# A written order for the first LayerNorm of a graph layer, part of it on GpSimd

## The chip, the cores and the metric

The kernel runs on one core of one Trainium2 chip. Its time is the device time of one execution in microseconds (us). Three runs of the kernel before took 1614.27, 1614.48 and 1616.7 us; their median, 1614.48 us, is what the change is measured against. A separate execution was profiled; its lines are quoted below.

The engines are named as the profile names them: PE (TensorE, matrix products and transposes), DVE (VectorE), ACT (ScalarE), POOL (GpSimd) and SP (SyncE, which only issues transfers).

## The reference, cut to what matters

```python
xn = _layernorm(x, axis=-1)                      # x: 6250 nodes x 256
x = x + _L0_gnn_ref(xn, src, dst, ...) + _L0_mix_ref(xn[None], ...)[0]
x = x + _L0_ffn_ref(_layernorm(x, axis=-1)[None], ...)[0]      # an LSTM over the 6250 rows

def _L0_gnn_ref(node_feats, src, dst, eps, W1, b1, W2, b2, gamma, beta):
    neigh = jax.ops.segment_sum(node_feats[src], dst, num_segments=n)   # 100000 edges
    h = (1.0 + eps) * node_feats + neigh
    h = jax.nn.relu(h @ W1 + b1) @ W2 + b2
    ...                                           # batch norm over the nodes
```

The mixing branch projects xn to q, k and v, normalizes k and v for each head, forms one 32x32 matrix a head from all nodes, and ends in a two-layer network with GELU.

## The kernel before, in words

**Layout.** The 6250 nodes lie as 125 rows by 50 steps: step s holds the nodes 50c + s. A "row tile" is one step, 125 partitions by 256 features, `xn[:, s, :]`. There are 50 of them.

**The first stage** (the pool `ln1`) does this. The edge lists `src` and `dst` come in on ACT's queue, are cast, transposed on PE and copied out as `si` and `drel` (L250 to L258). `x` comes in by five transfers of ten row tiles on SP's queue (each `move` makes two, of 112 and 13 partitions). Each group of ten is normalized: `bn_stats` and `bn_aggr` on DVE (L274, L275), the reciprocal root by the helper `rsqrt` (a Sqrt on ACT, L103, and a reciprocal with one Newton step on DVE, L105 to L109), the shift (L278), ten activations on ACT (L281), and a write of the group to `xn_d` in memory (L282). Then small DVE work makes, from the edges' first and last targets, the flag `within` and the bases `base_b` and `base_c` (L290 to L330). `to_columns` transposes the normalized tiles on PE, four at a time, and copies them to `xnT`, one half of the features on ACT (L120), the other on DVE (L122). Last come the centring of the k and v weights and their bias (L341 to L345), three products of a row of ones with bias rows (L348 to L352), and a transpose of the q weights (L358, L359). In this stage a scheduler orders the instructions of PE, DVE and ACT by their dependences.

**Between the stages**, L381 copies an index row to `iota_p`, and L383 (ACT) and L384 (DVE) write the nodes' own part, (1 + eps) times xn, into `sums`, one half of the features each: 6250 elements a partition, read in runs of 125 and written 50 elements apart. L386 clears the tail of `sums`.

**The edge stage** runs over the edges behind the first 34 groups, 162 groups of up to four tiles of 128 edges, 646 tiles in all. For each tile POOL issues an indirect gather of 128 rows of `xn_d` (L390) into a buffer `eg`, of which there are ten. For each group DVE makes `here`, the selections (L401); PE multiplies each gathered tile with them (L411, two products, each in two passes, so four records a tile); and DVE adds the result to a window of `sums` (L421). The order on PE, DVE and ACT is the written one here (`manual_schedule`). Into the slots between the products the loop puts other jobs: `count_job` counts the edges of the first 34 groups (its key is made on DVE at L623 and used on PE at L629), `kv_job`, `mix_job`, `gin_job` and so on. Slot 0 works on group 34; the selections of group 35 (slot 1) are asked for within slot 0.

**Afterwards** the batch norm is closed, and the LSTM runs over steps; its `residual` function normalizes one row tile at a time, with a `bn_stats` (L883), a `bn_aggr` (L885), an add (L887) and a power on POOL (L889) in a written order.

**Order of transfers.** Every engine works its own list in order; a transfer whose completion counter is still in use by an earlier transfer waits, and holds what stands behind it on its queue.

Of the kernel before, what the change touches and what calls it, by code (L numbers as in the profile page):

```python
# [23 lines left out]
P = 128  # L24
# [28 lines left out]
GRP = 10  # L53
BANK = 512
# [22 lines left out]
def gps_layer(ctx: ExitStack, tc: tile.TileContext, x, src, dst, cols, rows, kvln, wqkv, mw1, mw2, gw1, gw2,  # L77
# [34 lines left out]
    def to_columns(pool, tiles, dest):  # L112

        w = len(tiles) * NC
        for k in range(KD):
            pt = pool.tile([P, BANK], F32, name="mm")
            for i, t in enumerate(tiles):
                nc.tensor.transpose(pt[:, i * NC:(i + 1) * NC], t[:, k * P:(k + 1) * P], ident[:NC, :NC])
            if k == 0:
                nc.scalar.copy(dest[:, :, k, :], pt[:, :w].rearrange("p (s c) -> p s c", c=NC))  # L120
            else:
                nc.vector.tensor_copy(dest[:, :, k, :], pt[:, :w].rearrange("p (s c) -> p s c", c=NC))  # L122

    def by_step(t):

        return t[:N, :].rearrange("(c s) d -> c s d", s=NS)
# [27 lines left out]
    with ExitStack() as s1:  # L154
# [54 lines left out]
        with tc.tile_pool(name="ln1", bufs=2) as lp, tc.tile_pool(name="ps0", bufs=6, space=PSUM) as ps:  # L209
# [18 lines left out]
            for s0 in range(0, NS, GRP):  # L228
                move(nc.sync, xn[:, s0:s0 + GRP, :], by_step(x)[:, s0:s0 + GRP, :])
            row = lp.tile([1, NROW], F32, name="row", bufs=1)  # L230
            nc.scalar.dma_start(row, rows)
            nc.scalar.dma_start(w_qkv, wqkv.rearrange("(k p) m -> p k m", p=P))
            nc.scalar.dma_start(lnp, bass.AP(tensor=kvln.tensor, offset=kvln.offset,
                                             ap=[[0, P], [2 * D, 2], [1, 2 * D]]))
            nc.scalar.dma_start(w1, mw1.rearrange("(k p) m -> p k m", p=P))
            nc.scalar.dma_start(w2, mw2.rearrange("(k p) m -> p k m", p=P))
            nc.scalar.dma_start(g1, gw1.rearrange("(k p) m -> p k m", p=P))
            nc.scalar.dma_start(g2, gw2.rearrange("(k p) m -> p k m", p=P))
# [5 lines left out]

            nc.gpsimd.memset(counts, 0.0)


            for s, to in zip(tiled, (si, drel)):
                f = late[:, 2 * GE:2 * GE + (FULL + 1) * P].rearrange("p (b e) -> p b e", e=P)
                nc.vector.tensor_copy(f[:, :FULL, :], s[:, :FULL, :])  # L250
                nc.vector.tensor_copy(f[:NE % P, FULL, :], s[:NE % P, FULL, :])
                for b0 in range(0, FULL + 1, 4):
                    pt = ps.tile([P, BANK], F32, name="mm")
                    w = min(NE - b0 * P, BANK)
                    for b in range(b0, min(b0 + 4, FULL + 1)):
                        r = min(P, NE - b * P)
                        nc.tensor.transpose(pt[:, (b - b0) * P:(b - b0) * P + r], f[:r, b, :], ident[:r, :r])
                    nc.vector.tensor_copy(to[:, b0 * P:b0 * P + w], pt[:, :w])  # L258


            ends = lp.tile([P, 2, 2], F32, name="ends", bufs=1)
            for i, op in enumerate((ALU.min, ALU.max)):
                nc.vector.tensor_reduce(ends[:rows_g, i, :], dg[:rows_g], axis=AX.X, op=op)
            rows_c, each = COUNTED // 2, 2 * GT // CT
            pairs = lp.tile([P, 2, each], F32, name="pairs", bufs=1)
            for i, op in enumerate((ALU.min, ALU.max)):
                nc.vector.tensor_reduce(pairs[:rows_c, i, :], flat[:rows_c, :].rearrange("p (j e) -> p j e", j=each),
                                        axis=AX.X, op=op)

            for s0 in range(0, NS, GRP):  # L270
                mv = lp.tile([P, GRP, 2], F32, name="ln_mv")
                for i in range(GRP):
                    st = lp.tile([P, 6], F32, name="ln_st")
                    nc.vector.bn_stats(st[:NC], xn[:NC, s0 + i, :])  # L274
                    nc.vector.bn_aggr(mv[:NC, i, :], st[:NC])  # L275
                rs = rsqrt(lp, mv[:NC, :, 1], [NC, GRP], "ln")
                nc.vector.tensor_copy(ln_rs[:NC, s0:s0 + GRP], rs)
                nc.vector.scalar_tensor_tensor(ln_shift[:NC, s0:s0 + GRP], mv[:NC, :, 0], -1.0, rs, op0=ALU.mult,  # L278
                                               op1=ALU.mult)
                for s in range(s0, s0 + GRP):  # L280
                    nc.scalar.activation(xn[:NC, s, :], xn[:NC, s, :], AF.Identity, bias=ln_shift[:NC, s:s + 1],  # L281
                                         scale=ln_rs[:NC, s:s + 1])  # L282
                move(nc.sync, by_step(xn_d)[:, s0:s0 + GRP, :], xn[:, s0:s0 + GRP, :])

            nc.vector.tensor_scalar(ln_rs[:NC], ln_rs[:NC], 1.0, None, op0=ALU.add)
# [3 lines left out]
            fits = lp.tile([P, 2], F32, name="fits", bufs=1)  # L289
            nc.vector.tensor_sub(fits[:rows_g], ends[:rows_g, 1, :], ends[:rows_g, 0, :])  # L290
            nc.vector.tensor_scalar(fits[:rows_g], fits[:rows_g], float(W), None, op0=ALU.is_lt)
            nc.vector.tensor_mul(place[:rows_g], place[:rows_g], place[:rows_g])
            nc.vector.tensor_scalar(place[:rows_g], place[:rows_g], least(1) - least(0), least(0), op0=ALU.mult,
                                    op1=ALU.add)
            nc.vector.tensor_tensor(place[:rows_g], ends[:rows_g, 0, :], place[:rows_g], op=ALU.is_ge)
            nc.vector.tensor_mul(fits[:rows_g], fits[:rows_g], place[:rows_g])
            fit = lp.tile([P, 1], F32, name="fit", bufs=1)
            nc.vector.tensor_add(fit[:rows_g], fits[:rows_g, 0:1], fits[:rows_g, 1:2])

            fit_c = lp.tile([P, 2, each], F32, name="fit_c", bufs=1)  # L300
            nc.vector.tensor_sub(fit_c[:rows_c, 0, :], pairs[:rows_c, 1, :], pairs[:rows_c, 0, :])
            nc.vector.tensor_scalar(fit_c[:rows_c, 0, :], fit_c[:rows_c, 0, :], float(CW), None, op0=ALU.is_lt)
            nc.vector.tensor_scalar(fit_c[:rows_c, 1, :], pairs[:rows_c, 1, :], float(CN), None, op0=ALU.is_lt)
            nc.vector.tensor_mul(fit_c[:rows_c, 0, :], fit_c[:rows_c, 0, :], fit_c[:rows_c, 1, :])
            nc.vector.reduce_sum(place[:rows_c, 0:1], fit_c[:rows_c, 0, :], axis=AX.X)
            nc.vector.tensor_add(fit[:rows_c], fit[:rows_c], place[:rows_c, 0:1])
            pf = ps.tile([P, BANK], F32, name="mm")
            nc.tensor.matmul(pf[:1, :1], fit[:rows_g], ones[:rows_g, 0:1], start=True, stop=True)
            nc.vector.tensor_copy(within, pf[:1, :1])

            base_b = lp.tile([P, GROUPS], F32, name="base_b", bufs=1)
            for j in range(2):
                b = ends[:rows_g, 0, j:j + 1]
                pb = ps.tile([P, BANK], F32, name="mm")
                nc.tensor.transpose(pb[:, :rows_g], b.to_broadcast([rows_g, P]), ident[:rows_g, :rows_g])
                nc.vector.tensor_copy(base_b.rearrange("p (q j) -> p q j", j=2)[:, :, j], pb[:, :rows_g])
                nc.vector.tensor_copy(base_i.rearrange("p (q j) -> p q j", j=2)[:, :, j], pb[:1, :rows_g])

            base_c = lp.tile([P, PAIRS], F32, name="base_c", bufs=1)
            for j in range(each):  # L320
                b = pairs[:rows_c, 0, j:j + 1]
                pb = ps.tile([P, BANK], F32, name="mm")
                nc.tensor.transpose(pb[:, :rows_c], b.to_broadcast([rows_c, P]), ident[:rows_c, :rows_c])
                nc.vector.tensor_copy(base_c.rearrange("p (q j) -> p q j", j=each)[:, :, j], pb[:, :rows_c])
                nc.vector.tensor_scalar(c_base.rearrange("p (q j) -> p q j", j=each)[:, :, j], pb[:1, :rows_c],
                                        float(CN), None, op0=ALU.min)
            nc.vector.tensor_tensor(c_key.rearrange("p (q t) -> p q t", t=CT),
                                    drel[:, :COUNTED * GT].rearrange("p (q t) -> p q t", t=CT),
                                    base_c[:, :, None].to_broadcast([P, PAIRS, CT]), op=ALU.subtract)
            from_bases(drel, drel, base_b, ALU.subtract)  # L330

            for s0, n in CHUNKS:
                to_columns(ps, [xn[:NC, s, :] for s in range(s0, s0 + n)], xnT[:, s0:s0 + n])

# [827 lines left out]
```

## Time and profile before

| what | us |
|---|---|
| median of three runs | 1614.48 |
| the profiled execution, its own time | 1617.26 |
| its span, first to last instruction | 1615.2 |
| busy PE / DVE / ACT / POOL in the span | 1483.9 / 943.9 / 612.0 / 680.7 |
| the first L281 starts / the last group of L281 starts | 29.75 / 59.77 |
| first gather / last gather starts (L390) | 71.8 / 887.9 |
| PE busy with L411 | 389.1 |

Times in the profile's lists count from the start of the span. A row of the list in order of time gives the start, the duration, the engine, the source line, the operation, what is written from what, the shape, how often it stands there in a row, and, in brackets, how long the engine sat idle before it and what released it. A span of POOL or of a pipelined product is rough to some tens of nanoseconds.

### The profile page before, as it was taken

The numbers are of one execution on the slowest core, as the hardware profiler recorded it, in microseconds if no ns is written. First come the engines' busy times: TensorE is split into PE (matmuls) and PEld (weight loads), VectorE is DVE, ScalarE is ACT, GpSimd is POOL, SyncE is SP. The second block draws the span as 40 slices with busy tenths as digits, with TensorE's granted clock in tenths as the row PEclk, the third lists the DMA queues.
The fourth block names the chain that finished last, engine by engine and source line by source line (L and its number), as shares of the span: only waits on it lengthen the run. The fifth ranks groups of instructions, "written<-read, shape, count | busy, mean of one in ns | idle before, by whom it ended". The sixth has DMA issues, their size and how long they took to land. (4 is left out here: it accounts for less than half of the span.)

```text
span 1615.2 us, 31225 instructions
## 1 busy us (share of the span) xinstructions
PE 1483.9 (92%) x11312; PEld 1388.5 (86%) x11312; DVE 943.9 (58%) x3027; ACT 612.0 (38%) x1867; POOL 680.7 (42%) x714
## 2 busy tenths in 40 slices
PE   1789898999989999999999599999999999999984
PEld 1488788989888999999989599999999998888864
DVE  6789888888742222222222385555555557777777
ACT  2833333343312222233222255445554434444440
POOL 2177777777777777777777000000000000000005
PEclk9799999999999999999999799999999999999996
DMA  9533333333444554444444021111111002233315
GB/s 245 194 105 105 105 104 104 105 102 106 133 137 141 151 156 144 122 119 123 120 123 142 29 90 64 65 65 52 65 65 65 14 1 77 90 92 92 94 45 160
DMA packets 64645, 166.03 MB, mean 103 GB/s; under 512 B 14347, under 2 KB 29436, under 8 KB 63228
## 3 DMA queue, kind: packets, MB, share of 16 engines
q0 software_dynamic: 31008, 84.71, 18.4%
q1 hardware_dynamic: 29822, 75.08, 14.3%
q10 hardware_dynamic: 3648, 4.10, 1.1%
q8 instruction: 93, 1.52, 0.4%
q14 instruction: 74, 0.61, 0.1%
HBM read 130.56 MB, written 33.28 MB: 101 GB/s over the span
## 5 line engine op out<-in xcount | busy, mean ns | idle before, releaser
L390 POOL DMA_INDIRECT eg<-xn_d,si x646 | 620.5, 961 | 257.8 <-issue 99.3
L411 PE MATMUL pg<-here,eg 128*128 128x96 f32 x2584 | 389.1, 276 | 32.5 <-DMA eg<-xn_d,si 30.3
L411 PEld LDWEIGHTS pg<-here,eg 128*128 128x128 f32 x2584 | 358.2, 195 | 63.2 <-DMA eg<-xn_d,si 34.4
L962 ACT ACTIVATE gate<-pg,b_l 128x125 f32<-128x125 f32 x718 | 201.9, 366 | 230.4 <-PE pg L953 229.1
L421 DVE TENSOR_TENSOR sums<-sums,pg 128x192 f32 x162 | 57.3, 353 | 349.3 <-PE pg L411 202.9
L920 PE MATMUL pg<-yT,w_ih 128*128 128x125 f32 x1600 | 188.4, 276 | 0.0
L920 PEld LDWEIGHTS pg<-yT,w_ih 128*128 128x128 f32 x1600 | 184.1, 193 | 0.0
L953 PE MATMUL pg<-sums,w_hh 128*128 128x125 f32 x1568 | 183.1, 275 | 0.0
L953 PEld LDWEIGHTS pg<-sums,w_hh 128*128 128x128 f32 x1568 | 179.0, 192 | 0.0
L889 POOL TENSOR_TENSOR ln_r<-ln_v,minus_half 125x1 f32<-125x1 f32 x50 | 27.4, 552 | 350.9 <-DVE ln_v L887 314.0
L1091 POOL TENSOR_TENSOR xr<-xr,rest_t 125x1024 f32<-125x1024 f32 x8 | 22.9, 2899 | 312.3 <-DVEq L1036 312.3
L953 PE MATMUL pg<-h_w,w_hh 128*128 128x125 f32 x1248 | 145.6, 275 | 0.0
L613 ACT ACTIVATE sums<-mm,vec 128x125 f32<-128x125 f32 x100 | 36.4, 365 | 281.4 <-DVE sums L421 232.8
L953 PEld LDWEIGHTS pg<-h_w,w_hh 128*128 128x128 f32 x1248 | 143.0, 192 | 0.0
L597 PE MATMUL mm<-sums,g 128*128 128x125 f32 x800 | 116.8, 282 | 2.6 <-DVE counts L636 2.5
L608 PE MATMUL mm<-z,g 128*128 128x125 f32 x800 | 115.5, 284 | 0.8 <-DVE stats L614 0.6
L597 PEld LDWEIGHTS mm<-sums,g 128*128 128x128 f32 x800 | 103.8, 195 | 6.0 <-issue 2.3
L441 PE MATMUL mm<-m,xr 128*125 128x256 f32 x400 | 107.8, 395 | 0.6 <-DVE counts L636 0.6
L608 PEld LDWEIGHTS mm<-z,g 128*128 128x128 f32 x800 | 102.6, 197 | 1.2 <-DVE stats L614 0.8
L449 ACT ACTIVATE mm<-kv 125x512 f32<-125x512 f32 x50 | 30.1, 602 | 186.4 <-DVE kv L446 186.4
L968 DVE TENSOR_TENSOR new<-gate,gate 128x125 f32<-128x125 f32 x178 | 51.5, 289 | 65.2 <-ACT gate L962 60.3
L401 DVE TENSOR_TENSOR here<-counts,drel 128x384 f32<-128x384 f32 x162 | 89.4, 552 | 0.0
(238 smaller groups left out, 2164.6 us busy)
## 6 DMA issues: line engine op xcount, KB each, us to landing
x_d<-x_out SPq DMA_DIRECT2D x40, 500.0 KB
x_in<-x_d SPq DMA_DIRECT2D x40, 500.0 KB
eg<-xn_d,si POOLq DMA_INDIRECT x646
counts<-xn_d SPq DMA_DIRECT2D x16, 384.0 KB
xn<-in_x_dram SPq DMA_DIRECT2D x5, 1120.0 KB
xn_d<-xn SPq DMA_DIRECT2D x5, 1120.0 KB
m<-in_x_dram SPq DMA_DIRECT2D x50, 112.0 KB
out_dram<-o SPq DMA_DIRECT2D x12, 448.0 KB
```

The source lines that it names most:

```text
L390: nc.gpsimd.indirect_dma_start(out=g, out_offset=None, in_=xn_d[:], in_offset=bass.IndirectOffsetOnAxis(ap=at, axis=0))
L401: nc.vector.tensor_tensor(here[:, :n, :], iota[:, None, :W].to_broadcast([P, n, W]), drel[:, gi * GT:gi * GT + n, None].to_broadcast([P, n ...
L411: nc.tensor.matmul(pg[:, k, :], g[:, k * P:(k + 1) * P], here[:, i, :], start=(i == 0 and k == 0), stop=(i == n - 1), skip_group_check=True)
L421: nc.vector.tensor_add(window, window, pg)
L441: nc.tensor.matmul(pkv[:r, at], xnT[:, j, k, :], w_qkv[:, k, D:][:, at], start=(k == 0 and half == 0), stop=(k == KD - 1), skip_group_chec ...
L597: nc.tensor.matmul(p1[:, m, :], g1[:, k, m * P:(m + 1) * P], sums[:, k, at], start=(m == 0 and k == 0), stop=(k == KD - 1), skip_group_che ...
L608: nc.tensor.matmul(p2[:, a, :], g2[:, m, a * P:(a + 1) * P], z1[:, m, :], start=(a == 0 and m == 0), stop=(m == 2 * KD - 1), skip_group_ch ...
L613: nc.scalar.activation(sums[:, a, at], p2[:, a, :], AF.Identity, bias=col("gb2", a))
L920: nc.tensor.matmul(pg[:, SLOT[g], :], w_ih[:, k, block(g, a)], yT[:, k, s * NC:(s + 1) * NC], start=(i == 0 and k == 0), stop=False, skip_ ...
L953: nc.tensor.matmul(banks[a][:, SLOT[g], :], w_hh[:, k, block(g, a)], h[:, k, :], start=False, stop=(k == KD - 1), skip_group_check=True)
L962: nc.scalar.activation(gate[g], pg[:, SLOT[g], :], AF.Tanh if g == G else AF.Sigmoid, bias=bias(g, a))
L968: nc.vector.tensor_mul(new, gate[I], gate[G])
```

## The change

- **Groups.** x is loaded and normalized in groups of 10, 10, 10, 10, 5 and 5 row tiles (`LN_GROUPS`) where it was five of 10; each group is one pair of loads and one pair of writes to `xn_d`.
- **Order.** PE, DVE and ACT work this stage, too, in the order in which it is written. `bn_aggr` stands right behind its own `bn_stats`; all the flags, bases, keys and the weights' centring stand behind the last group.
- **Reciprocal root.** v to the power -0.5 on POOL (10 or 5 columns at once), with a Newton step on DVE; ACT's Sqrt and DVE's reciprocal go. One of the four `tensor_reduce` over the edges' targets stands behind each of the first four powers.
- **Normalization.** In a group of ten, ACT does seven tiles and POOL three; in a group of five, ACT four and POOL one.
- **Columns.** `to_columns` copies both halves on ACT. After the second, third and fourth group it is called for the tiles of the groups before; the remaining 22 tiles follow behind the bases.
- **Weights.** `w_qkv` is loaded on SP's queue right behind x; the other five weight loads move from ACT's queue to SP's, behind the last write to `xn_d`.
- **Own part.** It becomes a function that is called after the first gathers and the selections of group 34, inside the written order of the edge stage. ACT does 25 of the 50 steps of one half, DVE the other 25 and all 50 of the second half. In the list of DVE's instructions the selections of group 35 now stand behind it; they stood ahead of it.

```diff
-            if k == 0:
-                nc.scalar.copy(dest[:, :, k, :], pt[:, :w].rearrange("p (s c) -> p s c", c=NC))
-            else:
-                nc.vector.tensor_copy(dest[:, :, k, :], pt[:, :w].rearrange("p (s c) -> p s c", c=NC))
+            nc.scalar.copy(dest[:, :, k, :], pt[:, :w].rearrange("p (s c) -> p s c", c=NC))
...
-            for s0 in range(0, NS, GRP):
-                move(nc.sync, xn[:, s0:s0 + GRP, :], by_step(x)[:, s0:s0 + GRP, :])
+            for s0, n in LN_GROUPS:
+                move(nc.sync, xn[:, s0:s0 + n, :], by_step(x)[:, s0:s0 + n, :])
...
-            nc.scalar.dma_start(w_qkv, wqkv.rearrange("(k p) m -> p k m", p=P))
...
+            nc.sync.dma_start(w_qkv, wqkv.rearrange("(k p) m -> p k m", p=P))
...
+            with tc.manual_schedule(engines={mybir.EngineType.PE, mybir.EngineType.DVE, mybir.EngineType.Activation}):
...
+                for s0, n in LN_GROUPS:
+                    mv = lp.tile([P, GRP, 2], F32, name="ln_mv")[:NC, :n]
+                    for i in range(n):
+                        st = lp.tile([P, 6], F32, name="ln_st")
+                        nc.vector.bn_stats(st[:NC], xn[:NC, s0 + i, :])
+                        nc.vector.bn_aggr(mv[:, i, :], st[:NC])
+                    v, r, u = (lp.tile([P, GRP], F32, name=f"ln_{c}")[:NC, :n] for c in "vru")
+                    nc.vector.tensor_scalar(v, mv[:, :, 1], EPS, None, op0=ALU.add)
+                    nc.gpsimd.tensor_tensor(r, v, minus_half[:NC, :n], op=ALU.pow)
+                    for work in between[:1]:
+                        work()
+                    between = between[1:]
+
+                    nc.vector.tensor_mul(u, r, r)
+                    nc.vector.tensor_mul(u, u, v)
+                    nc.vector.tensor_scalar(u, u, -0.5, 1.5, op0=ALU.mult, op1=ALU.add)
+                    rs, shift_g = ln_rs[:NC, s0:s0 + n], ln_shift[:NC, s0:s0 + n]
+                    nc.vector.tensor_mul(rs, r, u)
+                    nc.vector.scalar_tensor_tensor(shift_g, mv[:, :, 0], -1.0, rs, op0=ALU.mult, op1=ALU.mult)
+                    mine = n - n // 3
+                    for s in range(s0, s0 + n):
+                        if s < s0 + mine:
+                            nc.scalar.activation(xn[:NC, s, :], xn[:NC, s, :], AF.Identity, bias=ln_shift[:NC, s:s + 1],
+                                                 scale=ln_rs[:NC, s:s + 1])
+                        else:
+                            nc.gpsimd.tensor_scalar(xn[:NC, s, :], xn[:NC, s, :], ln_rs[:NC, s:s + 1],
+                                                    ln_shift[:NC, s:s + 1], op0=ALU.mult, op1=ALU.add)
+                    move(nc.sync, by_step(xn_d)[:, s0:s0 + n, :], xn[:, s0:s0 + n, :])
+
+                    if n == GRP:
+                        columns_until(s0)
+                nc.sync.dma_start(lnp, bass.AP(tensor=kvln.tensor, offset=kvln.offset,
+                                               ap=[[0, P], [2 * D, 2], [1, 2 * D]]))
+                nc.sync.dma_start(g1, gw1.rearrange("(k p) m -> p k m", p=P))
+                nc.sync.dma_start(g2, gw2.rearrange("(k p) m -> p k m", p=P))
+                nc.sync.dma_start(w1, mw1.rearrange("(k p) m -> p k m", p=P))
+                nc.sync.dma_start(w2, mw2.rearrange("(k p) m -> p k m", p=P))
...
-        to = [sums[:, k, :N].rearrange("p (c s) -> p s c", s=NS) for k in range(KD)]
-        nc.scalar.activation(to[0], xnT[:, :, 0, :], AF.Identity, scale=ope)
-        nc.vector.scalar_tensor_tensor(to[1], xnT[:, :, 1, :], ope, iota_p[:, 0:1, None].to_broadcast([P, NS, NC]),
-                                       op0=ALU.mult, op1=ALU.add)
-        nc.vector.memset(sums[:, :, N:], 0.0)
+        def own_part():
+            to = [sums[:, k, :N].rearrange("p (c s) -> p s c", s=NS) for k in range(KD)]
+            half = NS // 2
+            nc.scalar.activation(to[0][:, :half], xnT[:, :half, 0, :], AF.Identity, scale=ope)
+            zero = iota_p[:, 0:1, None]
+            for k, s in ((0, half), (1, 0)):
+                nc.vector.scalar_tensor_tensor(to[k][:, s:], xnT[:, s:, k, :], ope, zero.to_broadcast([P, NS - s, NC]),
+                                               op0=ALU.mult, op1=ALU.add)
+            nc.vector.memset(sums[:, :, N:], 0.0)
...
             here = {COUNTED: selections(COUNTED)}
+            own_part()
             running, before, slot = [], None, 0
```

The flags, bases, keys, the weights' centring and the bias products are moved into the written order without a change of their own; their lines are left out above.

## The prediction

> **What bounds the kernel now.** I read first the busy tenths by slice and the costliest groups, then the list in order of time from 50 to 105 us, then the edge stage's beginning engine by engine.
>
> ```profile
> PE   1789898999989999999999599999999999999984
> ...
> POOL 2177777777777777777777000000000000000005
> ...
> L390 POOL DMA_INDIRECT eg<-xn_d,si x646 | 620.5, 961 | 257.8 <-issue 99.3
> ```
>
> PE is nearly full, yet POOL's seven tenths are the pace: its gathers follow each other all through the edge stage.
>
> ```profile
> 99.51 0.95 POOL L390 DMA_INDIRECT eg<-xn_d,si  x1 [0.30 <-PE pg L411]
> 100.76 0.95 POOL L390 DMA_INDIRECT eg<-xn_d,si  x1 [0.30 <-PE pg L411]
> 102.01 1.15 POOL L390 DMA_INDIRECT eg<-xn_d,si  x1 [0.30 <-issue]
> 103.47 0.95 POOL L390 DMA_INDIRECT eg<-xn_d,si  x1 [0.30 <-issue]
> ```
>
> One gather costs 0.95 + 0.30 = 1.25 us. 645 of them take 806 us; the first starts at 71.8 and the last at 887.9, 816 us. So only some 10 us of this stage are lost to anything else, and whatever shifts the gathers shifts the end by the same amount. A gather needs one of ten buffers: gather k (counted from 0) waits until PE has used tile k - 10. The beginning of the stage is therefore what to read.
>
> ```profile
> 71.80 1.14 POOL L390 DMA_INDIRECT eg<-xn_d,si  x1 [61.32 <-DVE m L359]
> 71.88 11.97 ACT L383 ACTIVATE sums<-xr,ope 128x6250 f32<-128x6250 f32 x1
> 71.97 11.90 DVE L384 SCALAR_TENSOR_TENSOR sums<-xr,ope,iota_p 128x6250 f32<-128x6250 f32 x1 [0.56 <-ACT iota_p L381]
> ...
> 83.84 0.22 DVE L386 MEMSET sums<- 128x192 f32 x1
> 83.97 0.92 DVE L623 TENSOR_TENSOR counts<-iota_p,counts 128x784 bf16<-128x784 f32 x1
> ```
>
> ```profile
> 84.94 0.49 PE L629 MATMUL mm<-counts 128*128 128x392 bf16 x1 [3.50 <-DVE counts L623]
> ...
> 99.25 0.66 PE L411 MATMUL pg<-here,eg 128*128 128x96 f32 x4
> ```
>
> The own part holds DVE for 12 us. PE gets through slot 0 and tile 4 (their selections were made at 57.13 and 58.62, inside the LayerNorm), then idles until the first count key at 84.89. POOL never notices: PE ends tile 15 at 99.91, and gather 25, which needs its buffer, starts at 103.47. That slack of 3.6 us is what a later DVE may use up free of charge.
>
> **The change, part by part.** Times are of the profiled execution.
>
> LayerNorm on DVE. The last group starts on ACT at 59.77 now. The written order is priced by the same chain in the LSTM's `residual`:
>
> ```profile
> 1106.01 0.43 DVE L883 BATCH_NORM_STATS2 ln_st<-xr 125x6 f32<-125x256 f32 x1
> 1106.47 0.18 DVE L885 BATCH_NORM_AGGREGATE ln_mv<-ln_st 125x2 f32<-125x6 f32 x1
> 1106.68 0.15 DVE L887 TENSOR_SCALAR ln_v<-ln_mv 125x1 f32<-125x1 f32 x1
> 1106.98 0.55 POOL L889 TENSOR_TENSOR ln_r<-ln_v,minus_half 125x1 f32<-125x1 f32 x1 [7.31 <-DVE ln_v L887]
> ```
>
> A `bn_aggr` behind its own `bn_stats` starts 0.46 after it; the next `bn_stats` may follow 0.09 later (22.54 to 22.63 in the list before), so 0.55 a tile, 0.12 more than now (two tiles in 0.87, a foreign operation included). Ten tiles take 9 x 0.55 + 0.46 + 0.21 = 5.62 to `v`. The power starts 0.30 later. Its price for ten columns is not in the trace: 0.55 for one column is the lower end; if all of it above the 0.10 of the smallest POOL fills grew with the columns it would be 4.6, the upper end. I take 1.0 (0.75 for five), near the row of the same operation. The target reduction beside it (1.20) covers 0.9 of that in the four groups of ten; in the groups of five nothing covers it. Then five dependent operations: 0.25 + 3 x 0.19 = 0.82 to the start of the shift, 0.09 to the next group. Ten: 5.62 + 1.34 + 0.82 + 0.09 = 7.87; five: 2.87 + 1.09 + 0.91 = 4.87. DVE can start earlier than now, at 16.15: the cast of `dst` follows the copies of `si`, which can end 0.5 behind PE's 12.81, at 13.3, no longer behind 2.3 us of reductions, and that chain took 2.83 (17.14 to 19.97). 16.15 + 4 x 7.87 + 2 x 4.87 = 57.4. Four activations at 0.50 end at 59.5. So the LayerNorm ends 5.3 us sooner than now (64.80).
>
> POOL's 14 normalizations are hidden by ACT: one tile of a 125x1024 add at 2.90 is 0.72 for 256, three are 2.2 against ACT's seven in 3.5. If they cost a full 2.9 each, a group of ten takes 8.7 and POOL becomes the bound; the last tile alone would add 0.9. ACT has 7 x 0.50 and up to six copies at 0.52, 6.6 us in 7.87, so DVE's 13 copies go to it free of charge; without that slack they would cost 12 x 0.52.
>
> Transfers. SP's loads of x no longer wait behind weights (8.7 us for `mw`, 4.9 for `wqkv`, 4.6 for `kvln` in SP's waits). 7.6 MB of x and edges at the 264 GB/s of 20 to 40 us are in by 31, each group before DVE wants it (24, 32, 40, 48): worth nothing by itself, as DVE sets the pace. Two more loads and two more writes cost SP 0.35 each, while it waits. The weights, 2.3 MB or 9 us, now follow the last write, up to about 73; they share the channels with the first gathers, are first used at 188 (L597), and b_r behind them on SP is first used past 91. `w_qkv` lands before 36 and is wanted at 66. The last write is 0.63 MB instead of 1.25: the way from issue to gather, 64.83 to 71.80, shrinks by 2.4, so the first gather comes at 59.6 + 4.5 = 64.1, 7.7 sooner.
>
> What DVE does then. It had hidden its small work in the LayerNorm; now that work is in one row. L312 waits for ACT's last activation, so all behind it starts at 59.6: flags 13 operations, mostly dependent at 0.18, 2.2; the product on PE 0.3; bases 12 copies 1.6; keys and `drel` 1.3; centring six operations at 0.62, 3.75; three key operations 0.6; selections 0.5. Sum 10.25, to 69.9. PE's 44 remaining transposes start behind the bases' transposes, at 63.3, and at 0.17 each (40 in 6.80 at 37.51) end at 70.8. Then the bias products and the q transpose:
>
> ```profile
> 64.97 2.07 PE L348 MATMUL mm<-row,ones 1*128 1x512 f32 x2
> ...
> 69.58 1.11 PE L358 MATMUL mm<-ident,m 128*128 128x128 f32 x4
> ```
>
> From 64.97 to the end of the copy behind them (L359, 71.42) that is 6.45, less 0.6 of transposes in between, 5.9, at a granted clock of 0.50 (60 to 70 us); at the 1.00 that stands over the dense transposes of 35 to 50 it would be about half, 2.9. Both rows bear on it; I take 4.4, to 75.2.
>
> [...]
>
> Own part. It waits for ACT's copy of `iota_p` (0.55), then DVE does 3125 + 6250 elements where it did 6250. At the row's 1.90 ns an element: 17.85. Lower end: both engines ran at the same rate side by side; if that is contention, DVE alone might go at the 1.2 ns of the contiguous L342 (0.66 for 512) once ACT has done its 6 us: 5.95 + 7.5 = 13.45. I take the row. 75.75 + 17.85 = 93.6.
>
> [...]
>
> Behind it come the memset (0.13), the selections of group 35 (0.5) and the key (0.92): 95.15, PE 0.05 later at 95.2, against 84.94: 10.3 late. Here the new wait bites: selections 35 stand behind the own part, PE's tile 4 behind them, and gather 14 behind tile 4. POOL, due there at 64.1 + 14 x 1.25 = 81.6, stands until about 94.5; the 7.7 won are used up in the ten buffers. From the key on, PE repeats its row from 84.94 to 99.91, and the gathers run at 1.25 again from gather 25 on, 10.3 - 3.6 = **6.7 us later** than now. All behind is unchanged. The profiled execution's span would be 1615.2 + 6.7 = 1621.9, its time 2.1 more; the median of the runs lies 2.8 below that execution's 1617.26, so 1614.5 + 6.7 = 1621.
>
> **The rivals.**
> - *The gathers' start decides* (faster). Then 7.7 are won: 1606.8. For it: POOL's even pace. Against: it needs the selections of group 35 by 81.6, and the sum has them at 94.3; even 13.45 for the own part gives 89.9. 6%.
> - *The own part was contended* (no change). 4.4 less: +2.3, 1616.8; with the power at 0.55 (0.7 less) and a full clock (1.5 less) +0.1, 1614.6. For it: equal rates on two engines whose clock need not be equal. Against: nothing else in the trace shows them slow each other. 24%; with a faster stretch somewhere else it ends below: 7% more.
> - *The power grows with its columns* (slower still). 4.6 for ten and 2.35 for five add 4 x 3.6 + 2 x 1.6 = 17.6: 1639. It decides from 0.9 us on, where the reduction no longer covers it. 10%.
> - That the change doesn't do what it says is out: the changed program's list has own part and selections in the order told.
>
> **How the numbers follow.** The forecast, 53%, lies at 1621, from 1618 (clock and power at their lower ends, 2.2 less) to 1625 (cold PE, 1.5, and a power of 1.5 us, some 2.5 more). 0.2%, 3.2 us, is about what a measurement tells from no change: faster ends at 1611.2, slower starts at 1617.7. Faster: 6 + 7 = 13%. Same: the contended case, 24%, less what ends over 1617.7, some 4%: 20%. Slower: the rest, 67%. The range 1611 to 1629 leaves out the first rival and most of the serial power.
>
> **What would show it.** In the changed profile: `bn_stats` 0.55 apart; the power's row near 1 us; the last activation near 59.5; first gather near 64; DVE's own part in two rows of 6 and 12 us ending near 93.6; PE idle up to there from about 80, with gather 14 standing until then; and gather 25 near 110. A second own-part row of about 7.5, or gather 14 before 85, would make the prediction wrong.

## The result and the profile after

Five runs of each kernel side by side: 1616.7 us (1614.27 to 1619.06) before, 1624.6 us (1623.08 to 1627.51) after. The ratio is 1.0052 with a 95% interval from 1.0036 to 1.0068: slower by 8.4 us, or 5.8 to 11.0. The profiled execution took 1623.08 us, its span is 1621.3.

The busy tenths by slice and the group of the gathers, from the page of the changed kernel:

```profile
PE   3478999999989999999999699999999999999985
...
POOL 4457777777777777777777100000000000000005
...
L420 POOL DMA_INDIRECT eg<-xn_d,si x646 | 621.8, 962 | 215.0 <-issue 103.8
```

POOL is busier in the first two slices (it now normalizes and raises to powers), its third slice has fallen from 7 to 5, and from the fourth on its sevens are as before: the gathers still set the pace. The idle time ahead of gathers has shrunk by 43 us: of the 61.3 ahead of the first one 6.2 are left, as POOL works in between, and later stalls add 12, 11 of them in one place. That one stall is what counts. It stands in POOL's list of the changed kernel (start, duration, instruction, in brackets the idle time before it and what ended it):

```profile
84.81 0.94 POOL L420 DMA_INDIRECT eg<-xn_d,si  x1 [0.30 <-issue]
96.92 0.94 POOL L420 DMA_INDIRECT eg<-xn_d,si  x1 [11.17 <-PE pg L441]
...
108.68 0.94 POOL L420 DMA_INDIRECT eg<-xn_d,si  x1 [1.14 <-PE pg L441]
109.93 0.95 POOL L420 DMA_INDIRECT eg<-xn_d,si  x1 [0.30 <-issue]
111.18 0.95 POOL L420 DMA_INDIRECT eg<-xn_d,si  x1 [0.30 <-PE mm L659]
112.43 0.95 POOL L420 DMA_INDIRECT eg<-xn_d,si  x1 [0.30 <-PE pg L441]
```

Gather 13 starts at 84.81, and gather 14 stands (waits for its buffer) for 11 us until PE has used tile 4. PE names what it waited for, and DVE's list what held that:

```profile
95.48 1.17 PE L441 MATMUL pg<-here,eg 128*128 128x96 f32 x4 [12.11 <-DVE here L431]
96.44 0.53 PE L659 MATMUL mm<-counts 128*128 128x392 bf16 x1
```

```profile
77.08 17.75 DVE L414 SCALAR_TENSOR_TENSOR sums<-xr,ope,iota_p 128x3125 f32<-128x3125 f32 x2 [0.57 <-ACT iota_p L407]
94.80 0.22 DVE L416 MEMSET sums<- 128x192 f32 x1
94.93 0.49 DVE L431 TENSOR_TENSOR here<-counts,drel 128x384 f32<-128x384 f32 x1
95.34 0.96 DVE L653 TENSOR_TENSOR counts<-iota_p,counts 128x784 bf16<-128x784 f32 x1
```

So the chain is the one foretold: own part, selections of group 35, PE's tile 4, gather 14. The table follows the delay. Times are us from the start of one profiled execution each; the last column is the ratio to the kernel before on the same chip, with its interval. "Changed, again" and what follows are explained in the next section.

| kernel | gather 0 | 14 | 25 | 40 | ratio |
|---|---|---|---|---|---|
| before | 71.8 | 89.5 | 103.5 | 122.5 | 1 |
| changed | 67.9 | 96.9 | 112.4 | 131.2 | 1.0052 (1.0036 to 1.0068) |
| changed, again | 67.9 | 97.7 | 114.0 | 133.5 | 1.0051 (1.0034 to 1.0069) |
| own part along rows | 67.9 | 97.1 | 112.3 | 131.1 | 1.0038 (1.0024 to 1.0052) |
| weights first | 67.9 | 97.6 | 113.7 | 133.1 | 1.0048 (1.0030 to 1.0065) |
| own part even | 67.9 | 91.1 | 106.1 | 125.0 | 1.0013 (1.0000 to 1.0026) |
| own part alone | 70.6 | 90.7 | 107.5 | 126.8 | 1.0010 (0.9997 to 1.0022) |
| power hidden | 62.5 | 92.6 | 109.4 | 128.5 | 1.0012 (0.9998 to 1.0026) |
| combined | 64.6 | 82.7 | 97.3 | 116.7 | 0.9947 (0.9928 to 0.9967) |
| combined, second | 62.0 | 82.3 | 97.8 | 116.7 | 0.9957 (0.9939 to 0.9974) |

Gather 0 comes sooner in every variant, and the times don't follow it; gather 40 orders the times nearly as the runs do. It is no exact measure. Two executions of the changed kernel lie 2.3 us apart there (131.2 and 133.5). The kernel before was profiled only beside the first result; on the two chips of the rows from "changed, again" on it ran 2.3 and 2.7 us longer than there (1618.99 and 1619.37 against 1616.7), so differences of these rows to its row carry some 2 us of that. Between the last gather and the end, these profiles differ by up to 6 us without order (721.1 to 727.4), and in the changed kernel the edge stage's 9.65 us at the last gather have become 6.1 at the end of the span.

### The profile page after: what moved, and what is told of

It reads as the page before. It is cut to its first block, busy times and chain, and to the rows that moved or that the text cites. A ratio compares the mean times of both kernels' runs of the same rounds, so it can differ in the third digit from the quotient of the medians.

```text
span 1621.3 us, 31247 instructions
## 1 busy us (share of the span) xinstructions
PE 1479.1 (91%) x11312; PEld 1392.5 (86%) x11312; DVE 952.1 (59%) x3011; ACT 606.1 (37%) x1862; POOL 699.5 (43%) x735
## 5 line engine op out<-in xcount | busy, mean ns | idle before, releaser
L627 PEld LDWEIGHTS mm<-sums,g 128*128 128x128 f32 x800 | 103.5, 194 | 6.3 <-issue 2.3
L431 DVE TENSOR_TENSOR here<-counts,drel 128x384 f32<-128x384 f32 x162 | 89.5, 553 | 0.0
```

Source lines behind the costliest of these rows:

```text
L431: nc.vector.tensor_tensor(here[:, :n, :], iota[:, None, :W].to_broadcast([P, n, W]), drel[:, gi * GT:gi * GT + n, None].to_broadcast([P, n ...
L627: nc.tensor.matmul(p1[:, m, :], g1[:, k, m * P:(m + 1) * P], sums[:, k, at], start=(m == 0 and k == 0), stop=(k == KD - 1), skip_group_che ...
```

## The experiments

Four runs came first, on a chip where the kernel before itself took 1759.89 us (median of 25). Their ratios hold; their microseconds don't compare with those above. No profile of the kernel before, and no run of the changed kernel, was taken there. The rest ran on two chips where the kernel before took 1618.99 and 1619.37.

**Own part, evenly** (the changed kernel with the own part as it was split before, in its new place):

```diff
-            half = NS // 2
-            nc.scalar.activation(to[0][:, :half], xnT[:, :half, 0, :], AF.Identity, scale=ope)
+            nc.scalar.activation(to[0], xnT[:, :, 0, :], AF.Identity, scale=ope)
             zero = iota_p[:, 0:1, None]
-            for k, s in ((0, half), (1, 0)):
-                nc.vector.scalar_tensor_tensor(to[k][:, s:], xnT[:, s:, k, :], ope, zero.to_broadcast([P, NS - s, NC]),
-                                               op0=ALU.mult, op1=ALU.add)
+            nc.vector.scalar_tensor_tensor(to[1], xnT[:, :, 1, :], ope, zero.to_broadcast([P, NS, NC]),
+                                           op0=ALU.mult, op1=ALU.add)
```

> The changed kernel with the own part divided evenly again: ACT all 50 steps of the first half of the features, DVE all 50 of the second. In the changed kernel's profile DVE's own part took 17.75 us (77.08 to 94.83), the first count key ended at 96.30, the gathers stood from 85.8 to 96.9, and gather 40 started at 131.2 (122.5 before). Theory A (DVE's length in the own part, in front of the selections and the key, sets when the gathers run again): DVE's own part 11.9, the key 5.9 earlier at 90.4, gather 40 at 125.3, the time 5.9 below the changed kernel's, so about 2.5 over before. Rival B (what is lost lies in the LayerNorm and in the first gather's competition with the weights): gather 40 stays near 131 and the time 8 over before. Rival C (side by side the two engines slow each other): each of the two parts takes longer than 11.9.

Measured: 1762.38 us, 1.0010 (0.9997 to 1.0023): 1.8 us over the kernel before (-0.5 to 4.0), near theory A's 2.5 and clear of rival B's 8.

**Selections ahead** (the changed kernel; the selections of group 35 stand ahead of the own part):

```diff
-            here = {COUNTED: selections(COUNTED)}
+            here = {g: selections(g) for g in (COUNTED, COUNTED + 1)}
...
-                if g + 1 < GROUPS:
+                if g + 1 < GROUPS and g + 1 not in here:
```

> The changed kernel with the selections of group 35 ahead of the own part, as they stood before the change; everything else stays. Theory A says that PE then does tile 4 before DVE is back and waits at the first count key instead: gather 14 at its even pace near 85 to 86, the key 0.4 earlier, gathers standing from gather 15 on, the time 0.5 below the changed kernel's, that is no gain that can be measured. Rival D (the selections' place alone is the new wait): the gathers keep their pace, gather 40 at 120 or earlier and the time no more than before's.

Measured: 1768.55 us, 1.0047 (1.0029 to 1.0065): 8.3 us over the kernel before (5.1 to 11.4), where the changed kernel lost 8.4 on its own chip. POOL's list of this variant:

```profile
87.59 0.95 POOL L420 DMA_INDIRECT eg<-xn_d,si  x1 [0.30 <-issue]
97.81 0.94 POOL L420 DMA_INDIRECT eg<-xn_d,si  x1 [9.28 <-PE pg L441]
```

Gather 14 is free (87.59) and gather 15 stands instead: PE gets through tile 4 and then waits for the first count key, which is behind the own part too. Gather 40 came at 135.3, not by 120 as rival D has it. Two waits stood behind one row; to remove one alone bought nothing that these runs can tell.

**Own part alone** (the kernel before, with only the own part in the change's place and split):

```diff
...
             here = {COUNTED: selections(COUNTED)}
+            own_part()
             running, before, slot = [], None, 0
```

> The kernel before with the own part alone changed: as a function behind the first gathers, in the written order, 25 steps of one half on ACT, 75 steps on DVE. Theory A: LayerNorm as before, first gather at 71.8, DVE's own part 17.8 instead of 11.9, selections of group 35 behind it (0.4), the first key at 84.9 + 6.4 = 91.3, less the slack of 3.6: gather 40 at 125.3, the time 2.8 over before. Rival B: the time of before.

Measured: 1760.99 us, 1.0005 (0.9994 to 1.0016): 0.9 us over the kernel before (-1.1 to 2.8). That decides neither way; theory A's 2.8 lies at the edge, rival B's 0 inside.

**Power hidden** (the changed kernel, where each group's end, from L287 on, is issued inside the next group's statistics):

```diff
-                for s0, n in LN_GROUPS:
+                def begin(s0, n, early):
...
                         nc.vector.bn_aggr(mv[:, i, :], st[:NC])
+                        if early and i == (4 if n == GRP else 2):
+                            end(*early)
```

> The changed kernel with the Newton step and the normalization of a group put behind the first five (three) bn_stats of the next group, so that the power on POOL (1.97 us for ten columns, 1.17 for five, DVE idle 0.95 to 1.35 beside it) runs under other work in five of the six groups. Theory A: LayerNorm ends 5.3 us earlier, all that follows on DVE too, the key 5.3 earlier at 91.0, gather 40 at 126, the time 5.3 below the changed kernel's, about 3 over before. A rival that has the x loads or ACT as the LayerNorm's pace would see less than 2.

Measured: 1762.54 us, 1.0000 (0.9988 to 1.0012). It lies 6 us below the variant with the selections ahead, the way that theory A has it, but its 3 us over the kernel before did not come out: 0.0 (-2.1 to 2.1) by the ratio, though the medians are 2.7 apart.

Why that chip was slower bears on whether these runs count. By stretches of 200 us (busy us and instructions of PE, its weight loads, DVE, ACT and POOL; then the granted clock, DMA share and GB/s), first the changed kernel, then the variant with the selections ahead:

```profile
200.00:400.00 200.00, 189.28 (x1389) 177.18 (x1388) 169.42 (x475) 74.25 (x213) 152.20 (x158) 0.97 0.36 104
400.00:600.00 200.00, 189.84 (x1432) 181.16 (x1432) 84.06 (x251) 49.10 (x146) 151.87 (x159) 0.97 0.48 140
```

```profile
200.00:400.00 200.00, 172.86 (x1169) 157.89 (x1169) 145.67 (x405) 61.64 (x175) 128.25 (x135) 0.93 0.31 89
400.00:600.00 200.00, 168.75 (x1166) 156.42 (x1164) 105.88 (x311) 49.23 (x141) 128.65 (x135) 0.92 0.37 106
```

There POOL issues 135 gathers where it otherwise issues 158: 1.48 us each on the mean instead of 1.27 (1.25 for most, more for some). This mean distance is called the pitch below; 1.25 stands for the faster one. The clock is lower and PE has more idle time as well; POOL's gathers wait for PE, so PE sets the pace. The gathers' data land as fast as elsewhere (a median of 2.4 us from issue to the last packet; the packets of their queue took 17.0% of a span of 1759.6 us in the own part alone there, and 18.4% of 1615.2 in the kernel before, 299 and 297 us). What makes PE wait there wasn't settled. It left open whether the delay is handed on only where POOL's even pace rules, so the main variants were run again, with the changed kernel itself.

**Changed, again.** No edit.

> The changed kernel once more, beside the variants that follow, so that they have it on their own chip. In the four variants before this the gathers followed each other every 1.48 us on the mean instead of 1.25, so PE and not POOL set the pace behind the stage's beginning. My theory (the own part's 17.75 us on DVE hold the first count key and with it PE for some 12 us, wherever the pace comes from): gather 14 at 97, and 8 us over the kernel before at either pace (+0.5%). Rival (only POOL's even pace hands the lost time on; where PE sets the pace its slack eats it): within 3 us of the kernel before where the gathers' pitch is 1.48, +8 where it is 1.25.

Measured: 1626.79 us against 1618.99, 1.0051 (1.0034 to 1.0069), at a pitch of 1.25. The rival on the pace can't be told by this run, but by the selections ahead, which is the changed kernel but for one move: at 1.48 it lost 0.47%, 5.1 us at least, and the rival allows 3. So the rival falls, unless the move itself cost several microseconds there, for which its list shows nothing. The changed kernel as it stands was not run at 1.48.

**Own part along rows.**

```diff
-            to = [sums[:, k, :N].rearrange("p (c s) -> p s c", s=NS) for k in range(KD)]
-            half = NS // 2
...
+            to = [sums[:, k, :N].rearrange("p (c s) -> p c s", s=NS) for k in range(KD)]
+            of = [xnT[:, :, k, :].rearrange("p s c -> p c s") for k in range(KD)]
+            half = 62
...
-                nc.vector.scalar_tensor_tensor(to[k][:, s:], xnT[:, s:, k, :], ope, zero.to_broadcast([P, NS - s, NC]),
+                nc.vector.scalar_tensor_tensor(to[k][:, c:], of[k][:, c:], ope, zero.to_broadcast([P, NC - c, NS]),
```

> The changed kernel with the own part walked along the rows of sums, so that it writes words that lie side by side and reads with steps of 1000 bytes, where the changed kernel reads side by side and writes with steps of 200 bytes. Same elements, same split. If the spread write is the price (1.9 ns an element against 1.2 in the contiguous operation): DVE's two rows take 3.8 and 7.5 instead of 6.05 and 11.87, gather 14 comes 6 us sooner than in the changed kernel, and the time is 6 us less than that of the changed kernel. If any spread access costs the same, read or write: rows and time as in the changed kernel (within 2 us).

Measured: 1624.08 us, 1.0038 (1.0024 to 1.0052), 2.7 us under the changed kernel beside it: between the 6 of the first theory and the 2 of the second. DVE's groups of this variant, shapes kept apart (instruction, count, then busy us and mean ns):

```profile
L415 DVE SCALAR_TENSOR_TENSOR sums<-xr,ope,iota_p 128x6250 f32<-128x6250 f32 x1 | 10.7, 10723 | 0.0
L415 DVE SCALAR_TENSOR_TENSOR sums<-xr,ope,iota_p 128x3150 f32<-128x3150 f32 x1 | 6.3, 6281 | 0.6 <-ACT iota_p L407 0.6
```

1.72 ns an element where the spread write took 1.90, and 1.99 beside ACT's row, where it took 1.94. The contiguous operation of the kernel before takes 1.29 (L342, 0.66 us for 512). So most of the price stays when the spread access is a read; the 7.5 us of the first theory are not to be had in this way. In this variant the row beside ACT's is the slower one; that was not followed up.

**Weights first** (the changed kernel; `w_qkv` and the five other weights back on ACT's queue, ahead of the LayerNorm).

```diff
-            nc.sync.dma_start(w_qkv, wqkv.rearrange("(k p) m -> p k m", p=P))
+            nc.scalar.dma_start(w_qkv, wqkv.rearrange("(k p) m -> p k m", p=P))
...
-                nc.sync.dma_start(w2, mw2.rearrange("(k p) m -> p k m", p=P))
```

> The changed kernel with w_qkv and the other weights issued on ACT's queue ahead of the LayerNorm, as in the kernel before. My theory (the loads' new place is worth nothing, as DVE paces the LayerNorm and not the arrival of x): last activation of the LayerNorm within 1 us of the changed kernel's 63.1, time within 2 us of it. Rival (x is late without it): DVE waits for x in the LayerNorm, first gather 3 to 8 us later; the key, and so the time, later by as much less the slack of 3.

Measured: 1625.29 us, 1.0048 (1.0030 to 1.0065); the last four activations start at 61.14 against 61.05, gather 0 at 67.88 against 67.89. The loads' new place is worth nothing that can be measured either way.

**Own part even, own part alone, power hidden, again**, the same three programs at a pitch of 1.25:

> The even split of the own part once more (half 0 on ACT, half 1 on DVE, everything else as changed), because on its first chip the gathers' pitch was 1.48 us and the kernel before had no profile there. At a pitch of 1.25: DVE's row ends 6 us sooner than the two rows of the changed kernel, gather 14 near 92 instead of 97 to 98, and the time 5 to 6 us less than the changed kernel, +2 to +3 over the kernel before. Rival (the key is held by what comes ahead of the own part): gather 14 within 2 us of the changed kernel's, time +6 to +8.

> The kernel before with the own part's new place and split alone, again for a chip with the pitch of 1.25. My theory: own part from 71.6 to 89.4, key 6.3 later than in the kernel before, less the slack of 3.6: +2 to +4, so that some 4 of the change's 8 us belong to the own part and the rest to the later start behind the new LayerNorm. Rival (the own part alone is the loss): +8. Rival (the slack takes all of it): within 1.

> The changed kernel with the power under the next group's statistics, again. The own part starts 4.6 sooner (72.5 against 77.1) as it did on the first chip, so gather 14 near 92.5 to 93 and the time 4 to 5 us less than the changed kernel, +3 to +4 over the kernel before. Rival (only the gathers' start counts): first gather 62 against 67.9, 5.9 less than the changed kernel. Rival (the wait for the power costs nothing, as the rest is held by the weights or the transposes): as the changed kernel.

Measured: 1620.43, 1620.68 and 1620.64 us against 1619.37; the ratios are in the table, and agree with those of the slower chip within their intervals. Each of the three is some 6 us below the changed kernel. DVE's and POOL's lists of the even split:

```profile
77.07 11.89 DVE L412 SCALAR_TENSOR_TENSOR sums<-xr,ope,iota_p 128x6250 f32<-128x6250 f32 x1 [0.57 <-ACT iota_p L407]
```

```profile
91.06 0.94 POOL L418 DMA_INDIRECT eg<-xn_d,si  x1 [5.31 <-PE pg L439]
```

The own part starts at 77.07 as in the changed kernel and ends 5.9 sooner; gather 14 stands 5.31 instead of 11.17. In the own part alone the same two rows of 17.75 as in the changed kernel start at 70.89, and gather 14 stands 2.70. PE's tile 5, at 85.2 before, starts at 90.9 in the even split (5.7 late, mostly by the late start), at 90.6 in the own part alone (5.4, by the split) and at 96.8 in the changed kernel: 11.6, about the sum.

Where the buffers forgive is seen at tile 12, whose buffer gather 22 needs (us; "late" against the kernel before):

| kernel | tile 12 ends | late | gather 22 starts | late |
|---|---|---|---|---|
| before | 97.67 | | 99.51 | |
| own part even | 102.10 | 4.4 | 102.37 | 2.9 |
| own part alone | 103.25 | 5.6 | 103.53 | 4.0 |
| changed | 108.41 | 10.7 | 108.68 | 9.2 |

Each of the three is forgiven the same 1.6 us, once, and not once for each cause; so both together must lose more than the sum of the two. In time the even split lost 2.1 us, the own part alone 1.6 and the changed kernel 8.4 (by the ratios). That gap is wider than 1.6, but each of these numbers has an interval of some 2 us either way; how much of the rest is real wasn't settled.

The power hidden expected 3 to 4 over the kernel before; 1.9 (-0.3 to 4.2) came out, with gather 14 where it was expected (92.56). Its gather 40 is 6.0 later than in the profile of the kernel before, more than the time shows; why wasn't settled.

**Combined**: the power hidden, each `bn_aggr` one tile behind its `bn_stats`, transposes after every group, bias products and q transpose ahead of the last transposes, the `+ 1.0` on `ln_rs` last, the own part even.

```diff
+                        if i < n:
+                            st = lp.tile([P, 6], F32, name="ln_st")
+                            nc.vector.bn_stats(st[:NC], xn[:NC, s0 + i, :])
+                        if last is not None:
+                            nc.vector.bn_aggr(mv[:, i - 1, :], last[:NC])
...
-                    if n == GRP:
-                        columns_until(s0)
+                    columns_until(s0)
...
-                nc.vector.tensor_scalar(ln_rs[:NC], ln_rs[:NC], 1.0, None, op0=ALU.add)
```

> A version meant to beat both: the power runs under the next group's statistics, each bn_aggr one tile behind its bn_stats, transposes follow every group, bias products and q transpose ahead of the last transposes, the + 1.0 on ln_rs behind all else so that nothing waits for the last normalization, and the own part evenly, half 0 on ACT and half 1 on DVE. From the rows: first gather near 58, own part from 65 to 77, gather 14 near 79 (89.5 in the kernel before), so 10 us less than the kernel before where the gathers' pitch is 1.25 (1607), and about as much less at the other pace. Rival (the pace of the edge stage is PE's from the start and a sooner first gather is not used): within 3 us of the kernel before.

Measured: 1611.93 us against 1618.99, 0.9947 (0.9928 to 0.9967): 8.6 us less than before where 10 were expected, 15 less than the changed kernel beside it. The own part ran from 66.2 to 78.1 and no gather waits for PE more than 0.3 us up to gather 21. Gather 0 came at 64.6 and not near 58, gather 14 at 82.7 and not near 79; ACT's list shows a part of it:

```profile
54.69 2.96 ACT L121 COPY xr<-mm 128x500 f32<-128x500 f32 x6
57.48 2.12 ACT L303 ACTIVATE xn<-xn,xr 125x256 f32<-125x256 f32 x4
```

Six copies of transposes, 3 us, stand ahead of the last four normalizations. What held up the rest of gather 0 wasn't taken apart, nor what each part of this version is worth.

**Combined, second**: those copies behind the normalizations, and the centring of the weights ahead of the copies of the bias products.

```diff
-                    columns_until(s0)
+                    if n == GRP:
+                        columns_until(s0)
...
+                columns_until(NS - GRP // 2 - 1)
                 p_bias = ps.tile([P, BANK], F32, name="mm")
```

> The best version so far with the last group's normalizations ahead of six copies of transposes that stood before them on ACT (2.8 us), and the centring of the weights ahead of the copies of the bias products. First gather near 62 instead of 64.6, no gather waits before 25, time 2 to 3 us less than that version (0.993 of the kernel before). If the gathers' start no longer decides but the own part's end (77.5, key 79.5): within 1 us of that version.

Measured: 1610.95 us against 1619.37, 0.9957 (0.9939 to 0.9974): no different from the first, where 2 to 3 us less were expected; the other forecast, within 1 us, came out. Gather 0 is 2.6 sooner (62.0), but the copies now end later, the own part starts at 68.35 instead of 66.20, and gather 14 stands 2.26. What was won at one end was given back at the other; gather 40 is at 116.7 in both.

## Why the prediction was right, and where its terms were off

The time was foretold at 1621 us and came out at 1624.6; 6.7 us over the kernel before were foretold, and 7.9 lie between the medians (8.4 by the ratio, 5.8 to 11.0). The mechanism stood as written: the own part's length on DVE holds PE and, through the ten buffers, POOL, and the sooner first gather is used up. The even split and the combined version show it from both sides. Term by term, from the changed kernel's profile, with its second profile ("changed, again") where that differs:

| step | foretold | measured |
|---|---|---|
| `bn_stats` to `bn_stats` | 0.55 | 0.53 |
| power, ten / five columns | 1.0 / 0.75 | 1.96 / 1.17 |
| last normalization ends | 59.5 | 63.1 |
| first gather | 64.1 | 67.9 |
| small DVE work from L312 on | 10.25 | 10.3 |
| 44 transposes | 7.5 | 6.1, second 7.3 |
| bias products to the copy behind the q transpose | 4.4 | 3.3 |
| own part | 75.75 + 17.85 | 77.08 + 17.75, second 77.90 + 17.74 |
| PE uses the first key | 95.2 | 96.4 |
| gather 14 | 94.5 | 96.9, second 97.7 |
| gather 25, over before | 6.7 | 9.0, second 10.6 |

*The power was the worst-sized term.* Its groups in the changed kernel, on POOL:

```profile
L282 POOL TENSOR_TENSOR ln_r<-ln_v,minus_half 125x10 f32<-125x10 f32 x4 | 7.9, 1964 | 22.9 <-DVE ln_v L281 22.9
L299 POOL TENSOR_SCALAR xn<-xn,xr 125x256 f32<-125x256 f32 x14 | 7.6, 554 | 6.8 <-DVE xr L292 6.8
L282 POOL TENSOR_TENSOR ln_r<-ln_v,minus_half 125x5 f32<-125x5 f32 x2 | 2.3, 1166 | 3.6 <-DMA xn_d<-xn 2.4 <-DVE ln_v L281 1.3
```

0.55 us for one column, 1.17 for five, 1.96 for ten: about 0.16 us for each further column. The rival on the power had the mechanism right, with a price 2.3 times too high (4.6). Past 0.9 us the target reduction no longer covers it, and DVE stands:

```profile
21.55 1.22 DVE L284 TENSOR_REDUCE ends<-xr 98x2 f32<-98x1024 int32 x1
23.73 0.17 DVE L287 TENSOR_TENSOR ln_u<-ln_r 125x10 f32<-125x10 f32 x1 [0.95 <-POOL ln_r L282]
```

A group of ten took 8.65 where 7.87 was foretold, a group of five 5.2 where 4.87 was: 3.8 us in all, and with a start 0.2 sooner the 3.6 by which the LayerNorm ended late. Only 1.3 of them reached the own part's start, because PE won about 2.5 back: its transposes took 0.14 each, and the bias products ran at full speed (1.09 for the pair that took 2.07 before; the granted clock is 1.00 from 72 to 74 us, and was 0.50 from 64 to 68 in the kernel before). For the bias products the prediction's lower figure, 2.9 at a granted clock of 1.00, was nearer to the measured 3.3 than the 4.4 taken. What the transposes won was luck. In this execution a transpose started every 0.21 us up to 69.3 us and every 0.11 from there on, though the granted clock reads 1.00 from 60 to 70 us; in the second profile the change came at 71.7 (the granted clock is 0.50 from 60 to 70 us and 0.84 from 70 to 80), so that all 44 took 7.29 and the own part started at 77.90. The 0.17 that the prediction took for one is such a mixture, too: in the kernel before, they started every 0.21 us up to 42.3 and every 0.11 after it.

*The slack was read at the wrong tile.* The prediction set tile 15's end at 99.91 against gather 25 at 103.47 and allowed 3.6. Every gather has its own tile, and the nearest pair counts. Tile 12, whose buffer gather 22 needs, in PE's list of the kernel before:

```profile
97.09 0.58 PE L411 MATMUL pg<-here,eg 128*128 128x96 f32 x4
```

and in the changed kernel:

```profile
107.83 0.58 PE L441 MATMUL pg<-here,eg 128*128 128x96 f32 x4
```

Before, it ends at 97.67, and gather 22 started at 99.51 (the first gather that the prediction shows): 1.8 us later, not 3.6. Of these the hand-over takes 0.27: in the changed kernel tile 12 ends at 108.41 and gather 22, which waited for it, starts at 108.68. So 1.6 us were free. Gathers 23 to 25 follow at 1.25: this is the last place where the delay was set. With 1.6 the sum would have been 8.7, and the time 1623.

*The rival of the contended own part* falls: DVE's second row, from 82.97 on, took 11.87, though ACT's row ended at 83.11: as slow alone as beside it. *The gathers' start decides* falls too: the power hidden had gather 0 at 62.5, 9.3 sooner than the kernel before, and was no faster than it; the even split has gather 0 where the changed kernel has it and took 6 us less. The price of nothing that the prediction set on the moved loads held (weights first), and POOL's normalizations took 0.55 a tile, 1.63 for three, under ACT's 3.5.

Three smaller readings were off. 0.66 us for 512 elements are 1.29 ns an element and not 1.2, so the lower end of the own part was 14.0 and not 13.45. 1621 less 2.2 is 1619, not the 1618 given as the lower bound. And the 6.97 us from issue to gather (64.83 to 71.80) don't measure the write, as the row quoted there puts the end of POOL's wait down to DVE's copy at L359; that 4.8 us passed from the last normalization to the first gather (63.1 to 67.9) where 4.5 were taken is in part luck.

## What to carry to other kernels

Where a producer runs ahead through a ring of buffers, a delay of the consumer is free up to the smallest distance between any buffer's release and its next use, over all of them, less the hand-over (1.8 less 0.27 us here), and it is forgiven once, not once for each cause. Before work is moved behind a wait, list what stands behind it on its engine: here the selections and the key were both behind the own part, so to free one of them won nothing measurable, to shorten the row 6 us. A sooner start is worth having only when the work that meets it is sooner too; the combined version, which moved both and more, is the one that won.

## What the runs showed of the hardware

- GpSimd's power costs by the column: 0.55, 1.17 and 1.96 us for 1, 5 and 10 columns of 125 partitions.
- After its idle time PE started at half speed here, and for how long varied between executions of one program. In the first profile of the changed kernel, behind 12.11 us of idle time, a tile's four matmuls took 1.0 to 1.2 us from 95.48 on and 0.58 from 100.22 on, 4.7 us later (the granted clock was 0.50 from 95 to 98 us and 1.00 from 100 to 102). PE's list of the same program in its second profile, where it resumed at 96.30:

```profile
101.27 1.00 PE L441 MATMUL pg<-here,eg 128*128 128x96 f32 x4
102.06 1.22 PE L471 MATMUL mm<-m,xr 128*125 128x256 f32 x4
103.12 0.58 PE L441 MATMUL pg<-here,eg 128*128 128x96 f32 x4
```

  By these rows it stayed at half speed for up to 6.8 us (the granted clock was 0.50 from 90 to 100 us and 0.88 from 100 to 110). Of the 1.6 us by which its gather 25 is later, 0.8 are PE's later start, which comes from the slower transposes above, and as much this. What sets that length was not shown.
- Chips differ: one ran the kernel before 9% slower (1759.89 against 1618.99 and 1619.37 us). The loss lay in the edge stage: behind the last gather its profiles take 722.7 to 725.9 us, as the others do. The ratios of the variants that ran on both kinds of chip agreed within their intervals.
